# Three hand-written issue lists laid out anew, with the second layer's weights loaded at the head of the DMA queue

## The chip, the cores and the metric

The kernel runs on one core of a Trainium2 chip. A core has five engines with instruction queues of their own: TensorE (PE; its weight loads are shown as PEld), VectorE (DVE), ScalarE (ACT), GpSimd (POOL) and SyncE (SP, which here only issues DMAs). Each runs its instructions in the order in which the program hands them over, and semaphores between the queues hold an instruction back until what it reads is there and what it overwrites has been read. The metric is the device time of one execution in microseconds; lower is better. The time of a kernel is the median of its runs.

## The reference

`x` is 16 x 512 x 512 (16 batches, 512 tokens, width 512), in float32. For each token three tables are looked up by index, and three conditions per batch go through a small two-layer network. Cut to what is computed:

```
h = ln(x, pw_g[pathway], pw_b[pathway]);  h = ln(h, cp_g[comp], cp_b[comp])
t = ln(x, tm_g[time], tm_b[time]);        s = ln(x, ms_g[scale], ms_b[scale])
m, n, r = x + mlp_ln(memory), x + mlp_ln(noise), x + mlp_ln(resource)      # one row per batch
w = softmax(aw)
cat = concat([w0*h, w1*t, w2*m, w3*n, w4*r, w5*s])                         # 16 x 512 x 3072
out = x + ln(silu(cat @ int_W1 + int_b1) @ int_W2 + int_b2, int_g, int_be)
```

`ln` is a layer norm with mean and variance over the 512 columns.

## The kernel before

The 8192 tokens are sorted by the pair (compartment, scale) and cut into 16 tiles of 512 tokens (four rows of 128, counted 0 to 3). Because tokens of one row mostly share their pair, the time and scale norms are folded into one product: the first layer becomes a sum of three products per row instead of six. They read `catX` (x turned, block X), `catV` (the normalised x turned, block V, against weights `vs` built for the row's pair), and `catH` (the pathway and compartment part, block H). The products of X and H are done by a seven-product scheme on halves (names `m7.tile.pair.k`; sums in `token_sum`), except for tile 0, which multiplies plainly (`lX`, `lV`, `lH`). A row that holds a border between two pairs gets an extra product against the difference (names `ex` for the product, `ey`/`ez` for turning its rows, `ea`, `ee`, `eo` for gathering, adding and writing the result). The second layer uses the seven products `q7`. Results are gathered and scattered with indirect DMAs on POOL, since tokens are sorted.

The order of the work is written out by hand. `ctx.enter_context(tc.manual_schedule())` (L642) means that every engine's queue has its instructions in program order, and the program order is that of three lists of piece names: `ORDER` (L21 to L44, tile 0 and what is done once), `WINDOW` (L47 to L62, run for tiles 0 to 14, with `p`, `c`, `n`, `m` for the tile before, this one, the next and the one after) and `LAST` (L64 to L78). `run` (L1463) goes through a list and calls each piece once; a piece that `ORDER` has done already for tile 0 or 1 is skipped in `WINDOW`. The setup code ahead of `ORDER` (indices, one-hot products for the sort, loads) has an order of its own, which is not touched. Where a list puts a piece ahead of another changes the order only on the engines that both use.

Pieces that the change or the prediction names, with their engine:

- `lw` (SP, `load_w2`, L1403): loads `int_W2`, 1 MB, into the tile `w2`. The tile holds the condition networks' first weights until then; they are read by the setup's products of L844. `lt`, `lh`, `lo` (SP, L1098 to L1106): loads of three small tables, of the first layer's H block into `wh_` (1 MB; `wh_` holds a condition weight until `h2.2` has read it) and of three vectors to all partitions. `do`, `ro` (SP): write the difference rows and the bias rows to DRAM, where the gathers find them.
- `h2`, `he`, `eh` (PE, ACT, PE), `cs`, `cp`, `cn`, `ct`, `ca`, `cm`, `cr`, `rp`, `rc`, `ro`: the condition networks' second layer, its norm, and the bias rows made of it. `tb` (PE): products of the tables with the weights, `wh_` among them.
- `wm` and `wl` (ACT): means of the second layer's weights, and their subtraction. `wz`, `wq` (DVE): sums of half weights for the seven-product schemes. `wh` (ACT): scales `wh_`.
- `g4` and `g6` (POOL, L987, L1002), `g5` (PE and ACT, L997), `bx`/`by`, `kd`, `gt`, `tk`, `xa`: find the extra rows and their tokens.
- per row: `gx`, `gh`, `gc`, `gr`, `ga` (POOL, gathers of x, of `pw` rows, of `cp` rows, of difference rows and of bias rows), `xs` (sums of a row of x), `f1`, `fs`, `fv`, `fp`, `f2`, `fn` (DVE, ACT, DVE, POOL, DVE, ACT: the two norms of block H; `f2` reads the `cp` rows), `nv` (ACT, the normalised x), `mt` (DVE, times the difference row), `sp` and `bd` (ACT and DVE, build `vs` for a row), `tx`, `tv`, `th`, `tz` (DVE, transposes), `sX`, `sV`, `sH`, `sZ` (SP, four DMAs of 64 KB each that spread a transposed row over the partitions), `xt`, `vt`, `ht` (PE, the transposes of tile 0) with `xv`, `vv`, `hv` (copies out of PSUM).
- `ha`, `hs` (DVE, ACT: first layer's end), `zs` (POOL, sums for the second layer), `kb` (ACT, puts the bias into PSUM), `kf`, `ku` (ACT) and `sf`, `sl` (DVE) take the second layer's products out of PSUM, `lq`, `lv`, `lp`, `lb` the last norm, `po` (POOL) the output's scatter. `e1` (ACT, L590): a first square root, ahead of those of the last tile.

The two `cp`-tagged buffers of the pool `gp` go round over `gc` and `gr` in the order of the list, so a gather waits until the piece that read its buffer two places earlier is done (`gc.0.1` for `ey.1`, for example).

Of the kernel before, what the change touches and what calls it, by code (L numbers as in the profile page):

```python
# [1537 lines left out]
```

## Time and profile before

| | |
|---|---|
| runs of the kernel | 930.51, 933.6, 935.81 us; median 933.6 |
| the profiled execution | 930.14 us, of which the span is 928.4 us |
| busy time of the span | PE 892.2 us, DVE 735.6, POOL 651.7, ACT 521.2 |
| from HBM and back | 100.48 MB read, 19.97 MB written |

A row of a timeline gives the start (us from the span's start), the time it covers, engine, line, operation, destination <- sources, shape and, in brackets, how long the engine was idle before it and what ended that. `xN` counts records: a float32 matmul leaves two. A line of the waits gives the engine, the tile and line that waited, what it waited for, the sum in us, how often, and the longest. A row of the windows gives the stretch, its length, the busy time of PE, PEld, DVE, ACT and POOL with the number of records, the granted clock of PE, the share of the 16 DMA engines, and GB/s. Where a helper records every operation, the lines are the helper's.

### The profile page before, as it was taken

How to read it: one execution, taken by the hardware profiler on the slowest of the kernel's cores; microseconds unless marked ns; L12 is line 12 of the kernel's file. 1: busy time of each engine (PE TensorE's matmuls, PEld its weight loads, DVE VectorE, ACT ScalarE, POOL GpSimd, SP SyncE). 2: the span in 40 equal slices, each digit the busy share in tenths (PEclk: the TensorE clock that was granted, in tenths of full speed). 3: DMA queues.
4: the chain of work that ended last, by engine and by line, in shares of the span. 5: the costliest groups of instructions: out<-in, count | busy, mean ns of one | idle time of the engine just before them, and what ended most of it. 6: DMA issues, size and time to landing. Idle time of an engine off the chain costs nothing. (4 is left out here: it accounts for less than half of the span.)

```text
span 928.4 us, 13749 instructions
## 1 busy us (share of the span) xinstructions
PE 892.2 (96%) x3617; PEld 642.1 (69%) x3617; DVE 735.6 (79%) x1360; ACT 521.2 (56%) x1261; POOL 651.7 (70%) x730
## 2 busy tenths in 40 slices
...
GB/s 277 224 142 226 191 263 191 194 217 193 243 177 232 202 208 195 214 199 207 204 201 243 175 243 190 222 188 220 182 209 200 200 229 182 224 198 167 168 37 111
DMA packets 88557, 185.40 MB, mean 200 GB/s; under 512 B 24324, under 2 KB 24388, under 8 KB 88476
## 3 DMA queue, kind: packets, MB, share of 16 engines
...
q14 instruction: 51, 0.42, 0.2%
q10 hardware_dynamic: 704, 0.08, 0.1%
HBM read 100.48 MB, written 19.97 MB: 130 GB/s over the span
## 5 line engine op out<-in xcount | busy, mean ns | idle before, releaser
L404 PE MATMUL p<-vs,catV 128*128 128x512 f32 x512 | 228.0, 593 | 0.9 <-PEq L1363 0.6
L404 PEld LDWEIGHTS p<-vs,catV 128*128 128x128 f32 x512 | 96.7, 190 | 104.6 <-issue 101.9
L452 PE MATMUL p<-wh__81,catH 128*128 128x256 f32 x480 | 111.1, 379 | 0.0
L376 ACT ACTIVATE pw<-pw,rsh 128x512 f32<-128x512 f32 x64 | 45.7, 718 | 101.4 <-issue 45.1
L452 PEld LDWEIGHTS p<-wh__81,catH 128*128 128x128 f32 x480 | 91.2, 190 | 12.4
L475 ACT ACTIVATE add<-add 128x512 f32<-128x512 f32 x64 | 40.2, 631 | 97.6 <-DVE add L472 74.8
L171 POOL DMA_INDIRECT xbs<-in_x,tok x64 | 68.0, 1063 | 35.6 <-DVE yb L634 19.6
L638 POOL DMA_INDIRECT out<-yb,tok x64 | 66.5, 1039 | 31.6 <-issue 17.9
L391 POOL TENSOR_TENSOR xbs<-xbs,rows 128x512 f32<-128x512 f32 x64 | 82.1, 1285 | 1.3
L171 POOL DMA_INDIRECT pw<-in_pw,i_pw x64 | 64.2, 1003 | 26.0 <-DVE rH L197 12.8
L171 POOL DMA_INDIRECT add<-rows,i_add x64 | 69.2, 1082 | 15.6 <-issue 15.6
L171 POOL DMA_INDIRECT cp<-cp_rows,i_cp x64 | 67.5, 1054 | 17.7 <-issue 14.3
L383 DVE SCALAR_TENSOR_TENSOR pw<-pw,sumsh,cp 128x512 f32<-128x512 f32 x60 | 43.9, 753 | 43.8 <-DMA cp<-cp_rows,i_cp 43.6
L350 ACT ACTIVATE junk<-pw 128x512 bf16<-128x512 f32 x60 | 37.7, 628 | 71.3 <-DVE pw L347 30.2
L346 DVE SCALAR_TENSOR_TENSOR pw<-xbs,sums,pw 128x512 f32<-128x512 f32 x60 | 59.9, 998 | 13.7 <-DMA pw<-in_pw,i_pw 11.2
L625 POOL TENSOR_TENSOR rsy<-vey,mhalf 128x4 f32<-128x4 f32 (+1 forms) x16 | 21.6, 1348 | 64.4 <-DVE vey L620 64.4
L317 ACT ACTIVATE xm<-xbs,nmx,rsx 128x512 f32<-128x512 f32 x64 | 48.9, 808 | 26.6 <-issue 21.4
L612 ACT ACTIVATE junk<-yb 128x512 bf16<-128x512 f32 x64 | 40.2, 628 | 38.2 <-DVE yb L576 27.9
L452 PE MATMUL u<-wt,catX 128*128 128x256 f32 x240 | 56.6, 379 | 0.4 <-DVE add L463 0.4
L452 PE MATMUL u<-wx__80,ss 128*128 128x256 f32 x240 | 56.7, 379 | 0.0
L452 PE MATMUL p<-wt,catH 128*128 128x256 f32 x240 | 56.7, 379 | 0.0
L452 PE MATMUL u<-wt,ss 128*128 128x256 f32 x240 | 56.7, 379 | 0.0
...
## 6 DMA issues: line engine op xcount, KB each, us to landing
...
```

What stands on the lines that cost most here:

```text
L171: nc.gpsimd.indirect_dma_start(dst, None, table, bass.IndirectOffsetOnAxis(ap=idx, axis=0), **kw)
L317: nc.scalar.activation(t, st["xb"][:, j, :], AF.Identity, bias=st["nm"][:, j : j + 1], scale=st["rs"][:, j : j + 1])
L346: nc.vector.scalar_tensor_tensor(h, st["xb"][:, j, :], st["sums"][:, 1, j : j + 1], h, ALU.add, ALU.mult)
L350: nc.scalar.activation(junk, x, AF.Identity, accum_out=sums[:, 0, k : k + 1])
L376: nc.scalar.mul(pw[:, :D], pw[:, :D], st.pop(("rs", j)))
L383: nc.vector.scalar_tensor_tensor(pw[:, :D], pw[:, :D], st["sh", j][:, 1], cp, ALU.add, ALU.mult)
L391: nc.gpsimd.tensor_add(st["xb"][:, j, :], st["xb"][:, j, :], rows[:, 2, :])
L404: nc.tensor.matmul(st["p1", g], st["c" + blk][:, g, c, :], m[:, c, :], start=(blk == first and c == order[0]), stop=(blk == last and c == ...
L452: nc.tensor.matmul(dst, m[:, c], at_["half1"][k][:, c], start=(k == 1 and c == 0), stop=(c == NC - 1), skip_group_check=True)
L475: nc.scalar.activation(st["add", g], st["add", g], AF.Silu)
L612: nc.scalar.activation(junk, yb[:, j, :], AF.Square, accum_out=st["ssy"][:, j : j + 1])
L638: nc.gpsimd.indirect_dma_start(out_rows[j], bass.IndirectOffsetOnAxis(ap=tok[:, j, w : w + 1], axis=0), yb[:, j, :], None)
```

## The change

All three lists hold the same names as before (380, 197 and 189), each once; only their order is new. No function is changed.

On SP, `lw` is now the first piece of `ORDER`, ahead of `lt`, `lh`, `lo`, `do` and `ro`; before, it stood behind both `ro`. `lh` now stands ahead of `lo`. On PE the order of tile 0 is now

```
before: sz h2.2 ax h2.1 h2.0 g5 eh.2 xt.0.1 dp xt.0.0 bx eh.0 cv xt.0.3 xt.0.2 eh.1 tb lX.0.0 vt.0.2 vt.0.1 ct
        lX.0.1 vt.0.0 cm vt.0.3 ht.0.0 rp.1 rp.0 ey.0 lV.0.1 ey.1 ht.0.2 ex.0 ey.2 lX.0.2 ex.2 ht.0.1 ey.3 ex.1 ...
after:  h2.0 h2.1 h2.2 ax sz xt.0.1 eh.2 eh.0 dp g5 xt.0.2 bx eh.1 xt.0.0 cv tb xt.0.3 vt.0.1 ct vt.0.2 vt.0.0
        cm ht.0.0 lX.0.0 rp.0 rp.1 vt.0.3 lX.0.1 ht.0.2 ey.0 lX.0.2 ey.1 ex.0 ey.2 lV.0.1 ex.1 ht.0.1 ey.3 ex.2 ...
```

On POOL, `g6` now stands ahead of `g4`, and the gathers `ea.1`, `ea.2` of the extras come earlier among the others. In `WINDOW`, on ACT `kf.p.1` stands ahead of `ku.p.0`, on DVE `sf.p.1` ahead of `sf.p.0`; on POOL `zs.p.0` stands behind `ga.c.2` and `fp.c.3`; on SP the rows of the next tile go `sV.n.3 sV.n.0 sV.n.2 sX.n.2 sX.n.0 sV.n.1 sX.n.1 sX.n.3`, where it was `sV.n.1 sV.n.0 sV.n.3 sV.n.2 sX.n.2 sX.n.0 sX.n.1 sX.n.3`. In `LAST`, the second layer's last products go 5, 7, 1, 6, 4, 2, 3 where it was 1, 7, 2, 5, 3, 6, 4, and `e1` stands behind the third root of the last tile. The diff, cut:

```diff
 ORDER = """
-    wk.1.3 se g4 fg wk.1.0 sz h2.2 ax wk.2.3 wk.1.1 pwi lt h2.1 h2.0 he.2 tt scl lo lh wk.2.1 pk xs.0.1 dk xs.0.3
-    wk.1.2 he.0 g5 eh.2 xt.0.1 dp g6 fl.3 he.1 dc xt.0.0 bx eh.0 cv xt.0.3 xt.0.2 eh.1 by xv.0.1 sp.0.1 xv.0.3
-    xv.0.2 ac xv.0.0 kd xs.0.0 xs.0.2 wk.2.2 cg wk.2.0 xe.0 cs gh.0.0 gt.0.3 gt.0.1 gt.0.2 gt.0.0 gh.0.2 xp.0
-    gc.0.0 cp f1.0.0 xm.0 tk.0 nv.0.2 fl.2 wm.4 nv.0.1 tb lX.0.0 vt.0.2 fl.0 vt.0.1 nv.0.0 nv.0.3 vv.0.1 vv.0.2
-    gx.e0.0 gt.1.3 gx.e0.1 gt.1.1 fs.0.0 cn f1.0.2 gt.1.0 gx.e0.2 ct fs.0.2 do xs.e0.0 gt.1.2 gx.e0.3 lX.0.1
-    vt.0.0 fl.1 ca fv.0.2 fv.0.0 cw tk.1 f2.0.0 vd.1 bd.0.1 gx.e1.2 gx.e1.3 gc.0.2 gr.e0.0 fp.0.2 gx.e1.1 fp.0.0
-    xs.e0.1 cm vt.0.3 xs.e0.2 xs.e0.3 fn.0.0 f2.0.2 xa.1 xe.e0 gr.e0.1 xp.e0 xm.e0 cr ht.0.0 rp.1 nv.e0.0 vv.0.3
-    vv.0.0 rc.1 ro.1 xa.0 xs.e1.1 va.0 mt.e0.0 hv.0.0 gh.0.1 gx.e1.0 rp.0 gx.1.0 ey.0 lV.0.1 nv.e0.1 rc.0 ar
-    mt.e0.1 xs.e1.0 fn.0.2 xs.e1.2 ez.0 nv.e0.2 nv.e0.3 xs.e1.3 ey.1 ht.0.2 gr.e0.2 f1.0.1 tx.1.0 xe.e1 mt.e0.2
-    fs.0.1 wl.4 sp.0.3 ex.0 ey.2 wb ro.0 lw sp.0.0 fv.0.1 gx.1.1 hv.0.2 ez.2 lX.0.2 ex.2 gc.0.1 ea.0 gx.1.2 gx.1.3
-    fp.0.1 gr.e0.3 gh.0.3 f2.0.1 ee.0 tx.1.1 bd.0.0 vd.0 mt.e0.3 eo.0 gc.0.3 xp.e1 va.1 fn.0.1 ez.1 xs.1.2 ht.0.1
-    ey.3 f1.0.3 fs.0.3 f2.0.3 xm.e1 fv.0.3 ea.2 gr.e1.0 ea.3 gr.e1.2 ea.1 gh.1.3 fp.0.3 ea.5 xs.1.3 ez.3 xs.1.0
-    xs.1.1 nv.e1.2 nv.e1.0 xe.1 ee.2 bd.0.3 mt.e1.0 mt.e1.2 ex.1 ey.6 ex.3 ey.4 ez.6 nv.e1.3 wm.0 nv.e1.1 ez.4
...
+    g6 fg wk.1.3 wk.1.0 g4 h2.0 h2.1 wk.1.1 dk lw h2.2 fl.1 xs.0.0 ax sz se wk.2.1 xs.0.2 wk.1.2 pwi he.1 he.0
+    he.2 xt.0.1 lt xs.0.1 wk.2.3 scl eh.2 eh.0 dp xs.0.3 lh gh.0.0 tt fl.2 xe.0 g5 lo xt.0.2 fl.3 gh.0.2 xp.0 bx
+    eh.1 xt.0.0 cv by xv.0.2 dc kd xm.0 wk.2.2 cs gt.0.0 gt.0.1 gt.0.3 gt.0.2 cp f1.0.0 fs.0.0 fv.0.0 cn cg nv.0.1
+    wm.4 nv.0.2 xv.0.0 sp.0.1 tb xt.0.3 vt.0.1 fl.0 ct vt.0.2 ca gt.1.3 gc.0.0 fp.0.0 tk.0 cw wk.2.0 f1.0.2 f2.0.0
+    nv.0.0 xv.0.3 ac vv.0.2 nv.0.3 xv.0.1 wl.4 fn.0.0 va.1 gx.e0.0 gx.e0.1 xa.0 xs.e0.0 pk vt.0.0 gt.1.2 gt.1.0
+    gx.e0.2 gx.e0.3 do gc.0.2 cm cr xs.e0.1 ht.0.0 lX.0.0 rp.0 rp.1 vt.0.3 xs.e0.2 xs.e0.3 hv.0.0 bd.0.1 fs.0.2
+    fv.0.2 f2.0.2 xe.e0 gt.1.1 gr.e0.0 gh.0.1 fp.0.2 gr.e0.1 xp.e0 tk.1 xm.e0 rc.0 fn.0.2 rc.1 nv.e0.0 nv.e0.1
+    mt.e0.0 f1.0.1 mt.e0.1 lX.0.1 ht.0.2 nv.e0.2 wh nv.e0.3 ey.0 ez.0 vv.0.0 gx.e1.3 gx.e1.1 ro.0 wb vv.0.1 ar
+    fs.0.1 gx.1.0 gr.e0.2 gx.1.2 gx.e1.0 xa.1 vd.0 lX.0.2 xs.e1.1 ey.1 mt.e0.2 vv.0.3 ro.1 xs.e1.0 ex.0 ea.0
+    gc.0.1 gx.e1.2 xs.e1.2 sp.0.0 xs.e1.3 ez.1 gx.1.3 xe.e1 fv.0.1 ee.0 gh.0.3 ey.2 fp.0.1 gr.e0.3 gx.1.1 xp.e1
+    bd.0.0 f2.0.1 tx.1.0 f1.0.3 mt.e0.3 tx.1.3 fs.0.3 tx.1.2 xs.1.2 xs.1.3 va.0 ez.2 fn.0.1 gc.0.3 eo.0 lV.0.1
+    ex.1 ht.0.1 ey.3 xm.e1 hv.0.2 fv.0.3 f2.0.3 gr.e1.0 ea.1 ea.2 gh.1.3 gr.e1.2 fp.0.3 nv.e1.0 xs.1.0 ez.3 xs.1.1
+    wm.0 fn.0.3 nv.e1.2 vd.1 ee.1 mt.e1.0 xe.1 mt.e1.2 hv.0.1 ex.2 ey.6 ex.3 ey.4 ez.6 nv.e1.1 nv.e1.3 wm.1
...
 WINDOW = """
-    kz.p.2 kz.p.1 ha.p.2 f1.c.2 kb.p.2 kz.p.0 ga.c.2 tz.p.3 lV.c.1 lV.c.0 m7.c.1.1 m7.c.0.1 kb.p.1 sh.c.1 kb.p.0
-    gc.c.2 gc.c.3 sp.c.3 hs.p.2 tz.p.2 bd.c.3 f1.c.3 fs.c.2 sp.c.2 xs.n.0 fs.c.3 fv.c.2 bd.c.2 f2.c.2 fv.c.3
-    f2.c.3 sZ.p.0 sZ.p.1 sZ.p.2 fp.c.2 ga.c.0 zs.p.0 fp.c.3 lV.c.3 q7.p.0.1 q7.p.0.2 q7.p.0.7 xs.n.1 fn.c.2 fn.c.3
-    kf.p.0 xs.n.2 zs.p.1 zs.p.2 q7.p.0.5 q7.p.0.6 ku.p.0 kf.p.1 tx.n.1 th.c.2 th.c.3 tx.n.3 r1.c.0 sZ.p.3 gh.n.0
-    zs.p.3 zs.p.4 sf.p.0 tx.n.2 sf.p.1 zs.p.5 xs.n.3 zs.p.6 q7.p.1.2 vd.n tx.n.0 r1.c.1 xe.n xp.n ga.c.1 ga.c.3
-    sH.c.3 sh.c.2 zs.p.7 sH.c.2 kz.p.3 q7.p.1.1 sl.p.0 sH.c.0 sH.c.1 q7.p.0.3 q7.p.0.4 kb.p.3 kf.p.2 va.n sf.p.2
-    sl.p.1 xm.n q7.p.1.5 q7.p.1.7 nv.n.1 nv.n.3 lq.p.0 kf.p.3 f1.n.0 tv.n.3 tv.n.1 sf.p.3 q7.p.1.6 lV.c.2 q7.p.1.4
...
-    m7.c.0.4 m7.c.0.3 fs.n.1 sp.n.0 fn.n.0 f2.n.1 r5.c.1 fv.n.1 r3.c.0 th.n.0 r2.c.1 ha.c.1 lb.p.3 ha.c.0 m7.c.1.7
-    m7.c.1.4 gx.m.2 gx.m.0 po.p.0 gx.m.1 sh.c.0 fp.n.1 po.p.1 gh.n.2 sh.c.3 po.p.2 hs.c.1 hs.c.0 fn.n.1 tz.c.1
-    r3.c.1 tz.c.0 th.n.1 ha.c.3 sV.n.1 sV.n.0 sV.n.3 sV.n.2 sX.n.2 sX.n.0 sX.n.1 gh.n.3 gx.m.3 sX.n.3 hs.c.3
-    po.p.3 bd.n.0
+    kz.p.1 lV.c.1 lV.c.0 kz.p.0 kz.p.2 ha.p.2 gc.c.2 f1.c.2 tz.p.3 kb.p.0 kb.p.1 kb.p.2 sh.c.1 gc.c.3 ga.c.0
+    m7.c.0.1 m7.c.1.1 sp.c.3 hs.p.2 tz.p.2 bd.c.3 f1.c.3 fs.c.2 xs.n.0 sp.c.2 fs.c.3 fv.c.2 f2.c.2 bd.c.2 fv.c.3
+    f2.c.3 sZ.p.0 sZ.p.1 sZ.p.2 fp.c.2 ga.c.2 fp.c.3 zs.p.0 lV.c.3 q7.p.0.2 q7.p.0.1 q7.p.0.7 fn.c.2 xs.n.1 fn.c.3
+    kf.p.0 zs.p.1 zs.p.2 q7.p.0.5 q7.p.0.6 q7.p.1.2 q7.p.1.1 xs.n.2 kf.p.1 r1.c.0 tx.n.1 th.c.2 th.c.3 tx.n.3
+    tx.n.0 ku.p.0 sf.p.1 sf.p.0 gh.n.0 zs.p.3 sZ.p.3 zs.p.4 zs.p.5 tx.n.2 vd.n r1.c.1 xs.n.3 sH.c.1 zs.p.6 kz.p.3
+    sH.c.2 sH.c.0 xe.n sl.p.0 xp.n ga.c.3 ga.c.1 sh.c.2 zs.p.7 sH.c.3 q7.p.0.4 q7.p.0.3 kb.p.3 va.n kf.p.2 sf.p.2
+    sl.p.1 xm.n f1.n.0 q7.p.1.5 q7.p.1.7 q7.p.1.6 lV.c.2 nv.n.1 nv.n.3 kf.p.3 tv.n.1 tv.n.3 sf.p.3 q7.p.1.4
...
+    m7.c.1.5 m7.c.0.5 m7.c.0.6 m7.c.1.6 m7.c.0.4 m7.c.0.3 f1.n.1 lb.p.0 lb.p.2 lb.p.1 r5.c.0 r2.c.0 r5.c.1 u4.c.1
+    f2.n.0 m7.c.0.7 fs.n.1 fn.n.0 ha.c.0 r2.c.1 th.n.0 r3.c.0 f2.n.1 fv.n.1 ha.c.1 lb.p.3 m7.c.1.3 m7.c.1.7
+    m7.c.1.4 po.p.0 gx.m.2 sh.c.0 po.p.1 gx.m.0 gh.n.2 fp.n.1 po.p.2 sh.c.3 hs.c.0 hs.c.1 fn.n.1 sp.n.0 tz.c.1
+    th.n.1 r3.c.1 gh.n.3 sV.n.3 sV.n.0 sV.n.2 sX.n.2 sX.n.0 sV.n.1 tz.c.0 ha.c.3 sX.n.1 gx.m.3 gx.m.1 sX.n.3
+    hs.c.3 bd.n.0 po.p.3
 LAST = """
...
-    m7.c.0.4 m7.c.0.3 q7.p.1.1 q7.p.1.7 q7.p.1.2 q7.p.1.5 r3.c.1 ha.c.2 r3.c.0 ft.p.1 ha.c.1 ha.c.3 ha.c.0 hs.c.2
-    hs.c.3 hs.c.1 hs.c.0 kf.p.2 kf.p.3 tz.c.3 tz.c.1 e0 tz.c.2 tz.c.0 sf.p.3 sf.p.2 ft.p.0 po.p.1 zs.p.6 zs.p.7 w2
-    po.p.0 sZ.c.0 q7.p.1.3 q7.p.1.6 q7.p.1.4 l2.c.0 e1 ku.p.1 sl.p.2 sl.p.3 yg.p.2 yg.p.3 la.c.0 lq.p.3 lq.p.2
-    sd.p.3 sd.p.2 lq.c.0 sd.c.0 sZ.c.1 sZ.c.3 sZ.c.2 rv.p.2 ft.p.2 rv.p.3 yg.c.0 rv.c.0 ft.p.3 ft.c.0 l2.c.1
-    l2.c.3 l2.c.2 po.p.2 po.p.3 sh.c.2 po.c.0 la.c.1 lq.c.1 sd.c.1 yg.c.1 rv.c.1 ft.c.1 la.c.3 la.c.2 lq.c.2
-    sd.c.2 lq.c.3 sd.c.3 po.c.1 yg.c.2 rv.c.2 ft.c.2 rv.c.3 yg.c.3 ft.c.3 po.c.2 po.c.3
...
+    m7.c.0.4 m7.c.0.3 q7.p.1.5 q7.p.1.7 q7.p.1.1 r3.c.1 ha.c.2 ft.p.0 r3.c.0 ft.p.1 ha.c.3 ha.c.1 ha.c.0 hs.c.3
+    hs.c.2 hs.c.1 hs.c.0 kf.p.2 kf.p.3 tz.c.3 tz.c.1 e0 tz.c.0 tz.c.2 sf.p.3 w2 po.p.1 sh.c.3 zs.p.7 po.p.0 sZ.c.0
+    q7.p.1.6 q7.p.1.4 q7.p.1.2 q7.p.1.3 l2.c.0 ku.p.1 sl.p.2 sl.p.3 sf.p.2 yg.p.3 yg.p.2 la.c.0 lq.p.3 lq.p.2
+    sd.p.3 sd.p.2 lq.c.0 sd.c.0 sZ.c.2 sZ.c.1 sZ.c.3 rv.p.2 rv.p.3 ft.p.2 rv.c.0 ft.p.3 yg.c.0 ft.c.0 l2.c.2
+    l2.c.1 l2.c.3 po.p.2 po.p.3 po.c.0 la.c.2 la.c.1 lq.c.1 sd.c.1 lq.c.2 sd.c.2 rv.c.1 yg.c.1 ft.c.1 la.c.3
+    yg.c.2 yg.c.3 rv.c.2 ft.c.2 e1 lq.c.3 sd.c.3 po.c.1 rv.c.3 ft.c.3 po.c.2 po.c.3
...
```

37 lines of the change are left out of this document (18 added, 19 removed).

## The prediction

> **What bounds the kernel now.** I read the page first, for the span, and then the busy time of the engines in three stretches: the rest of the start behind the setup code (38 to 78 and 78 to 120 us, where the list ORDER runs) and the long stretch in which the windows run. Columns: PE, PEld, DVE, ACT and POOL busy, granted clock, DMA share, GB/s.
>
> ```profile
> span 928.4 us, 13749 instructions
> ```
>
> ```profile
> 38.00:78.00 40.00, 35.86 (x228) 18.04 (x227) 30.69 (x99) 25.81 (x70) 29.28 (x34) 0.91 0.50 155
> 78.00:120.00 42.00, 35.49 (x95) 16.01 (x95) 28.13 (x53) 29.84 (x66) 25.97 (x27) 0.92 0.74 233
> 120.00:905.00 785.00, 777.65 (x3051) 575.85 (x3049) 634.04 (x1129) 439.43 (x1057) 555.75 (x569) 1.00 0.72 200
> ```
>
> From 120 us on PE is idle for 7.35 of 785 us at the full clock: nothing that only changes an order can win more than that there, and since no operation goes, PE's work stays. The start is different: PE is idle 4.1 us in the first of its stretches and 6.5 us in the second, at clocks of 0.91 and 0.92. Next, whom PE waited for over the whole run, and PE's timeline where the long waits lie.
>
> ```profile
> PE px L1350 <- DVE pre L1343: 3.4, 1, 3.4
> PE ptH L1201 <- ACT pw L376: 3.1, 2, 2.2
> PE pq_0b L546 <- DVE yb L565: 2.5, 12, 0.2
> PE pq_0b L546 <- POOL yb L532: 2.1, 4, 0.8
> PE px L1350 <- issue: 1.4, 1, 1.4
> ...
> PE pq_1b L546 <- DVE yb L565: 1.1, 1, 1.1
> PE ptH L1201 <- DMA adde<-rows,i_x: 0.9, 1, 0.9
> ```
>
> ```profile
> 94.58 0.66 PE L1201 MATMUL ptH<-ident,pw 128*128 128x128 f32 x4 [0.84 <-ACT pw L376]
> 98.59 1.11 PE L1350 MATMUL px<-ident,pre 128*128 128x128 f32 x4 [3.36 <-DVE pre L1343]
> 99.50 5.55 PE L1365 MATMUL pe<-wt,catZ 128*128 128x512 f32 x8
> 105.48 3.67 PE L1365 MATMUL pe<-wt,catZ 128*128 128x512 f32 x8 [0.42 <-PEq L1348]
> ...
> 125.94 14.28 PE L404 MATMUL p<-wh__81,catH 128*128 128x512 f32 x32
> ```
>
> The pair 0.84 and 3.36 us is one event, and its cause is read from the queues: SP's timeline, POOL's, and DVE's.
>
> ```profile
> 35.37 0.51 SPq L1053 DMA_DIRECT2D in_order<-catZ  x1
> ...
> 41.78 0.37 SPq L1103 DMA_DIRECT2D wh__81<-in_int_W  x1
> ...
> 81.58 0.40 SPq L1404 DMA_DIRECT2D w<-in_int_W  x1
> ```
>
> ```profile
> 82.63 0.95 POOL L171 DMA_INDIRECT cp<-cp_rows,i_cp  x1 [0.83 <-PE ptH L1201]
> ```
>
> ```profile
> 92.88 0.75 DVE L381 SCALAR_TENSOR_TENSOR pw<-pw,sumsh,cp 128x512 f32<-128x512 f32 x1 [4.93 <-DMA cp<-cp_rows,i_cp]
> ...
> 95.24 2.70 DVE L265 SCALAR_TENSOR_TENSOR vs<-wt,sct,vs 128x512 f32<-128x512 f32 x4
> 97.85 0.69 DVE L1343 TENSOR_TENSOR pre<-xme,pre 128x512 f32<-128x512 f32 x1
> ```
>
> The second layer's weights (lw, 1 MB) go out at 81.58 us. The gather of the `cp` rows (gc.0.1) is issued at 82.63 and its first reader (f2.0.1) starts at 92.88, after 4.93 us in which DVE did nothing. Behind it in DVE's order stand a weight build (bd.0.0, 2.70 us) and the product that ey.3 transposes (97.85 us), so PE loses 0.84 us at ht.0.1 and 3.36 us at ey.3. The DMA share and the clock (last three columns) in slices of 2 us:
>
> ```profile
> 36.00:38.00 2.00, 2.00 (x38) 1.10 (x35) 0.55 (x4) 1.98 (x4) 0.44 (x3) 1.00 0.31 24
> ...
> 52.00:54.00 2.00, 2.00 (x8) 0.80 (x7) 1.64 (x11) 2.00 (x5) 0.97 (x1) 0.56 0.69 252
> ...
> 90.00:92.00 2.00, 2.00 (x6) 0.91 (x5) 0.00 (x0) 0.00 (x0) 1.56 (x2) 1.00 0.91 348
> ...
> 98.00:100.00 2.00, 1.41 (x5) 1.25 (x6) 1.95 (x3) 0.79 (x3) 0.10 (x1) 0.50 0.10 39
> ```
>
> While the gather is late the DMA engines are full (348 GB/s); at 36 to 38 us they move 24 GB/s. Behind the idle 3.36 us the clock is 0.50.
>
> **The change part by part.** *lw moves* from behind the bias rows (ro) to the head of SP's list. It needs only that the first condition products (L844) have read the same buffer, long past, so it goes out behind the L1053 issue, at about 36 us. It is one issue (0.40 us on SP) and 1 MB: 3.0 us at the 348 GB/s of the full row, so landed near 40 us. It passes lt, lo, lh, do and both ro on SP's queue. The three lt loads are short and wait 0.40 us more. The gathers of the first tile's x are issued from 38 us on, so at most 2 us of the transfer meet them; I take nothing, and 2 us as the upper end. lh still waits for h2.2 and now stands ahead of lo; its tile is read here:
>
> ```profile
> 57.35 0.63 PE L1264 MATMUL pb<-wh__81,room 128*32 128x512 f32 x3
> ```
>
> That is 15.6 us behind the 41.78 of the issue; two products ahead of h2.2 and the third megabyte take a third of it. Cover gone, each microsecond would be one of PE.
>
> [...]
>
> *What the move frees.* Without the megabyte beside it, and with the bias rows (ro) earlier too, gc.0.1 should land well inside its old 9.3 us (82.63 + 0.95 to 92.88). In the new list, from the end of ey.1 (which frees its buffer) PE has ex.0, lV.0.1 and ex.1 to do before ht.0.1, by the 14.28 us for four such blocks some 10.7 us. Against it stands the longer of two ways: the gather's issue and landing, or, on ACT and DVE, some copies, sp.0.0 (about as long as bd.0.0), bd.0.0 itself (2.70 us); then f2.0.1 (0.75 us) and one row operation of ACT. I put that at 8.5 us, an estimate, so slack of 2 us. ey.3 has under 1 us by the same count. I take both stalls as gone: 0.84 + 3.36 us. Then PE has no gap ahead of ex.1, which ran 5.55 us against the 3.67 us of its like: 1.9 us, and 0.45 us on ey.3's own transposes (1.11 against 0.66). The 0.9 us at ht.0.3 is late extra rows; the gathers ea.1 and ea.2 go earlier in the new list; I take 0.7 of it. The half microseconds that PE's sequencer spends on skipped blocks stay. Sum for 78 to 120 us: −(0.84 + 3.36 + 1.9 + 0.45 + 0.7) = −7.3 us; bounds −9 (all of the idle time and the clock's loss) and +1.
>
> [...]
>
> *The rest of ORDER, to 78 us.* One move speaks against the change: g6 now stands ahead of g4 on POOL.
>
> ```profile
> 46.91 2.54 POOL L1003 TENSOR_SCALAR room<-room,off 14x896 f32<-14x896 f32 x1
> ```
>
> So the segment rows come 2.54 us later, and PE's g5, with everything PE has behind it (bx, eh.1, xt.0.0, the table products), waits up to that long. For it: fn.0.0 goes ahead of the extras' sums on ACT, where ht.0.0 waited 2.2 us; the extra products' chain (cm, cr, rp) starts before lX.0.0 and lX.0.1 instead of behind; ht.0.2 goes ahead of ey.0, where PE stood 1.4 us. But ht.0.0 now stands ahead of both lX, with less of PE's work to hide f2.0.0. I take 0, with −3 (the 2.2 and part of the 1.4) and +3 (the 2.54 and a little) as ends.
>
> *WINDOW*, 14 full times. kf.p.1 and sf.p.1 go ahead of ku.p.0 and sf.p.0, so the half that PE overwrites next is read one ACT copy and one DVE sum sooner: the 12 waits on L565 go, −2.5 us. zs.p.0 now stands behind ga.2 and fp.3 on POOL; it waits for the spread of Z anyway, which hides both; cover gone, the 2.1 us on L532 grow. Bounds −4.5 and +3.
>
> In SP's list V's row 1, which PE reads first in the next window, becomes the sixth of eight rows instead of the first:
>
> ```profile
> 523.04 10.02 SPq L205 DMA_DIRECT2D catV<-rV  x16
> 533.16 14.03 SPq L205 DMA_DIRECT2D catX<-rX  x16
> ```
>
> ```profile
> 545.76 2.74 PE L404 MATMUL p<-vs,catV 128*128 128x512 f32 x6
> ```
>
> At 10.02/16 = 0.63 us each the 24th transfer is issued 15 us behind 523.04, at 538 us; PE reads row 1 at 545.76. Some 5 us of slack are left after the landing: no cost.
>
> *LAST.* The end's 1.1 us on L565 halves, since products 1, 6 and 4 now stand between 5 and 3, but 6 then waits for ACT's copy: −0.5 us. The root's table load (e1) leaves its idle place:
>
> ```profile
> 901.90 1.28 ACT L592 ACT_TABLE_LOAD   x1
> ```
>
> It now falls on the roots of tile rows 2 and 3 of the tile before, whose outputs are not the last; hidden, 1.28 us if not. −0.5 us in all, bounds −1.5 and +1.3.
>
> **Sum:** −7.3 + 0 − 2.5 − 0.5 = −10.3 us on the profiled execution, which took 930.14 us (span 928.4 and 1.7 us around it): 919.8. The runs shown go from 930.51 to 935.81 with the median 933.6, so that execution is 3.5 us under the median; a median of new runs should stand above 919.8 by some of this. I take about a third, 921 us.
>
> **The rivals.**
>
> *The head is won and partly given back* where the next waits lie: tile 1's rows X and V stand in SP's list behind the extras' last rows (eo.4 to eo.7), and those behind POOL's gathers ea. If POOL, whose gathers cost about a microsecond each, comes no earlier than before, the 28 transfers behind eo (28 × 0.63 = 17.6 us) reach PE several microseconds late, and 3 to 6 us of the 10.3 return: 925. For it: POOL is busy 25.97 of 42 us without its gaps. Against: its waits there were for the same late gathers.
>
> *Nothing measurable:* the stalls at 94 to 99 us only move, because ey.3 has under 1 us of slack, or the 2.54 us of g6 reach ht.0.0 whole. Then 2.5 + 0.5 us are left, or less: 930 to 933, I say 931.
>
> *Slower:* V's row 1, now sixth. Its 5 us of slack hang on X's rows 2 and 0 being issued at once; if their wait for the token sums' readers holds the queue, each further microsecond is paid 14 times. Up to 5 us it costs nothing; with the start's gain spent, a delay of 6.5 us gives +21 − 10 = +11 us, 945. Against it: the 14.03 us for X's 16 rows hold 4 us of waiting in all, and these belong to the two rows that the last half products still read.
>
> **How the numbers follow.** Forecast 0.62, given back 0.18, nothing 0.12, slower 0.08. About 0.5% (4.7 us) is what a measurement of this kernel can tell from no change. The forecast is faster whole; of "given back" I count four fifths faster; of "nothing" all as same: faster 0.76, same 0.16, slower 0.08. The forecast's own range, with the bounds of its terms taken together, is 914 to 928; with the next two cases 913 to 932.
>
> **What would show it.** Right: no wait over 1 us at ey.3 (L1350) and none of DVE on `cp` near 80 to 95 us; the L404 block of 32 records on `wh` starting 6 to 11 us earlier than 125.94; no row of L546 waiting 12 times for L565; the clock 1.00 where it was 0.50. Wrong: PE waits for the gathers of x (L171) before 50 us; a wait of L404 on `catV` in every window; the block on `wh` where it was, or the gap between it and the first half products grown.

## The result, and the profile after

The changed kernel takes 921.85 us (median of four runs from 921.23 to 922.6); the kernel before, beside it, 932.06 (928.84 to 935.81). The ratio is 0.989, with a 95% interval from 0.985 to 0.993: 10 us less, the predicted time within 1 us. The profiled execution took 922.05 us. The sum came out; two of its terms were mis-sized and a third was missing, so part of the nearness is luck. The windows of the changed kernel, with the columns of the prediction:

```profile
span 920.3 us, 13553 instructions
```

```profile
38.00:78.00 40.00, 36.81 (x235) 17.56 (x234) 30.13 (x93) 27.46 (x72) 30.65 (x35) 0.87 0.63 201
78.00:120.00 42.00, 39.44 (x107) 17.86 (x108) 32.92 (x69) 33.64 (x71) 32.16 (x32) 1.00 0.74 220
```

From 78 to 120 us PE is busy 39.44 us instead of 35.49, at the full clock instead of 0.92. The waits of PE over the whole run:

```profile
PE pq_0b L546 <- POOL yb L532: 4.3, 5, 1.6
PE pt L1295 <- issue: 2.0, 1, 2.0
PE p L404 <- DVE vs L265: 1.7, 1, 1.7
PE pq_0a L546 <- ACT yb L556: 1.2, 1, 1.2
...
PE ptH L1201 <- DVE pw L346: 0.8, 1, 0.8
...
PE px L1350 <- issue: 0.5, 1, 0.5
```

The 3.4 us at L1350 (ey.3), the 3.1 us of L1201 on ACT's `pw` and the 12 waits on L565 are gone, as forecast. Not in the sum: L532 grew from 2.1 to 4.3 us, and 2.0, 1.7 and 1.2 us are new.

To see where the time went, every trace is cut into four stretches by five points: the issue of L1053 on SP (the last of the setup, at 34.90 to 35.96 us in the 14 traces), the start of the block on `wh` (L404), the start of the second window's first block on `vs`, the start of the last block (L487), and the end. Before, from SP's and PE's timelines (the other two points of before stand in the prediction):

```profile
191.15 7.03 PE L404 MATMUL p<-vs,catV 128*128 128x512 f32 x16
241.59 7.03 PE L404 MATMUL p<-vs,catV 128*128 128x512 f32 x16
...
905.22 13.97 PE L487 MATMUL p<-w,catV 128*128 128x512 f32 x32
```

After:

```profile
35.87 0.51 SPq L1053 DMA_DIRECT2D in_order<-catZ  x1
```

```profile
118.84 14.28 PE L404 MATMUL p<-wh__81,catH 128*128 128x512 f32 x32
...
144.46 3.67 PE L404 MATMUL p<-vs,catV 128*128 128x512 f32 x8 [0.37 <-issue]
...
152.80 1.10 PE L546 MATMUL pq_0a<-w2t,yb 128*128 128x256 f32 x4 [1.22 <-ACT yb L556]
...
185.88 7.03 PE L404 MATMUL p<-vs,catV 128*128 128x512 f32 x16
235.87 7.03 PE L404 MATMUL p<-vs,catV 128*128 128x512 f32 x16
...
896.96 13.97 PE L487 MATMUL p<-w,catV 128*128 128x512 f32 x32
```

| stretch, us | before | after | difference |
|---|---|---|---|
| start: L1053 to the block on `wh` | 90.57 | 82.97 | −7.60 |
| first window, from there | 65.21 | 67.04 | +1.83 |
| the windows behind it, to L487 | 714.07 | 711.08 | −2.99 |
| the end | 23.18 | 23.34 | +0.16 |

These sum to −8.6; the setup ended 0.5 us later in this execution (35.87 against 35.37), and the spans differ by 8.1. The medians differ by 10.2.

### The profile page after: what moved, and what is told of

Read it like the earlier page. It is cut to its first block, busy times and chain, and to the rows that moved or that the text cites. A ratio compares the mean times of both kernels' runs of the same rounds, so it can differ in the third digit from the quotient of the medians.

```text
span 920.3 us, 13553 instructions
## 1 busy us (share of the span) xinstructions
PE 887.0 (96%) x3617; PEld 642.2 (70%) x3617; DVE 726.6 (79%) x1360; ACT 520.4 (57%) x1261; POOL 669.5 (73%) x730
## 5 line engine op out<-in xcount | busy, mean ns | idle before, releaser
L404 PE MATMUL p<-vs,catV 128*128 128x512 f32 x512 | 228.1, 593 | 4.0 <-DVE vs L265 1.7
L404 PEld LDWEIGHTS p<-vs,catV 128*128 128x128 f32 x512 | 96.6, 190 | 108.4 <-issue 100.8
L638 POOL DMA_INDIRECT out<-yb,tok x64 | 76.9, 1201 | 31.3 <-issue 15.1
L376 ACT ACTIVATE pw<-pw,rsh 128x512 f32<-128x512 f32 x64 | 45.6, 714 | 92.9 <-DVE pw L383 53.7
L171 POOL DMA_INDIRECT cp<-cp_rows,i_cp x64 | 74.4, 1162 | 14.5 <-issue 12.8
L625 POOL TENSOR_TENSOR rsy<-vey,mhalf 128x4 f32<-128x4 f32 (+1 forms) x16 | 23.6, 1474 | 83.1 <-DVE veh L368 70.1
L171 POOL DMA_INDIRECT xbs<-in_x,tok x64 | 66.0, 1031 | 22.0 <-issue 18.2
L171 POOL DMA_INDIRECT pw<-in_pw,i_pw x64 | 63.0, 984 | 25.1 <-issue 12.2
L171 POOL DMA_INDIRECT add<-rows,i_add x64 | 66.9, 1045 | 19.3 <-issue 19.3
L383 DVE SCALAR_TENSOR_TENSOR pw<-pw,sumsh,cp 128x512 f32<-128x512 f32 x60 | 45.6, 761 | 39.7 <-DMA cp<-cp_rows,i_cp 31.2
L372 POOL TENSOR_TENSOR rsh<-veh,mhalf 128x1 f32<-128x1 f32 x64 | 48.5, 758 | 14.9 <-DVE veh L368 11.6
L346 DVE SCALAR_TENSOR_TENSOR pw<-xbs,sums,pw 128x512 f32<-128x512 f32 x60 | 46.0, 767 | 12.5 <-DMA pw<-in_pw,i_pw 6.8
L452 PE MATMUL u<-wx__80,ss 128*128 128x256 f32 x240 | 54.5, 379 | 0.0
L452 PEld LDWEIGHTS u<-wx__80,catX 128*128 128x128 f32 x240 | 45.6, 190 | 12.7 <-issue 6.9
```

The costliest lines, as they stand in the source:

```text
L171: nc.gpsimd.indirect_dma_start(dst, None, table, bass.IndirectOffsetOnAxis(ap=idx, axis=0), **kw)
L346: nc.vector.scalar_tensor_tensor(h, st["xb"][:, j, :], st["sums"][:, 1, j : j + 1], h, ALU.add, ALU.mult)
L372: nc.gpsimd.tensor_tensor(rs, st.pop(("ve", j)), mhalf[:, :1], ALU.pow)
L376: nc.scalar.mul(pw[:, :D], pw[:, :D], st.pop(("rs", j)))
L383: nc.vector.scalar_tensor_tensor(pw[:, :D], pw[:, :D], st["sh", j][:, 1], cp, ALU.add, ALU.mult)
L404: nc.tensor.matmul(st["p1", g], st["c" + blk][:, g, c, :], m[:, c, :], start=(blk == first and c == order[0]), stop=(blk == last and c == ...
```

## The experiments

Each kernel has the same pieces in another order; all compute the whole result. The same four stretches, from one trace each, with the medians and ratios to the kernel before (95% interval). Times of before in these comparisons: 931.0 to 932.0. A trace is of a single execution; three of them lie 4 us or more from their medians: 940.52 us ("two swaps"), 935.47 ("zs.p.0 ahead") and 925.0 ("changed, again").

| kernel | median | ratio | start | first window | windows | end |
|---|---|---|---|---|---|---|
| before, `lw` first | 928.96 | 0.997 (0.995 to 0.999) | 84.8 | 65.2 | 718.7 | 23.1 |
| before, new ORDER | 930.24 | 0.998 (0.996 to 1.001) | 85.5 | 67.5 | 715.5 | 23.1 |
| before, new WINDOW and LAST | 925.64 | 0.992 (0.989 to 0.995) | 90.4 | 65.0 | 710.2 | 23.3 |
| before, two swaps | 932.17 | 1.002 (0.999 to 1.005) | 91.6 | 65.2 | 722.9 | 23.1 |
| before, POOL new | 949.7 | 1.020 (1.017 to 1.023) | 88.0 | 65.2 | 734.8 | 23.1 |
| changed, again | 920.62 | 0.988 (0.984 to 0.993) | 85.7 | 66.8 | 711.9 | 23.3 |
| changed, `lw` back | 925.69 | 0.991 (0.988 to 0.994) | 86.7 | 66.9 | 711.8 | 23.3 |
| changed, swaps undone | 920.51 | 0.986 (0.982 to 0.990) | 85.4 | 67.8 | 707.5 | 23.3 |
| changed, zs.p.0 ahead | 943.77 | 1.014 (1.009 to 1.018) | 82.0 | 66.4 | 726.1 | 23.3 |
| changed, POOL old | 959.21 | 1.030 (1.026 to 1.034) | 81.9 | 67.7 | 748.2 | 23.4 |
| changed, gx in order | 919.65 | 0.988 (0.984 to 0.993) | 82.0 | 66.5 | 710.1 | 23.4 |
| changed, gx, wl, wq early | 919.62 | 0.987 (0.983 to 0.990) | 85.6 | 66.4 | 706.9 | 23.3 |

### The weights' load alone

```diff
 ORDER = """
-    wk.1.3 se g4 fg wk.1.0 ...
+    lw wk.1.3 se g4 fg wk.1.0 ...
...
-    ... ey.2 wb ro.0 lw sp.0.0 ...
+    ... ey.2 wb ro.0 sp.0.0 ...
```

> The kernel before, with one item moved: lw stands first in ORDER. The prediction's theory (the second layer's megabyte held up the gather gc.0.1): DVE's wait for cp ahead of f2.0.1 shrinks from 4.93 us to under 1, the waits of 0.84 and 3.36 us at ht.0.1 and ey.3 go, the clock behind them stays at 1.00, and the first window's block on wh starts 4 to 6 us earlier than 125.94; time 4 to 6 us under the kernel before. Rival (the order of the lists did it, the megabyte's place is nothing): the 4.93 us stays above 3, the block stays within 1 us, time the same.

DVE's row of f2.0.1 and PE's of ey.3 in this trace:

```profile
87.99 0.81 DVE L381 SCALAR_TENSOR_TENSOR pw<-pw,sumsh,cp 128x512 f32<-128x512 f32 x1 [1.16 <-DMA cp<-cp_rows,i_cp]
```

```profile
94.67 0.66 PE L1350 MATMUL px<-ident,pre 128*128 128x128 f32 x4 [1.18 <-DVE pre L1343]
```

The reader is to see the 4.93 us of DVE shrink to 1.16 (a little over the microsecond expected) and the 3.36 of PE to 1.18 with nothing else changed; the start is 5.8 us shorter. Three more traces below have the old ORDER with the load in its old place: DVE's wait is 4.21 us in the one with the new WINDOW and LAST, and PE's at ey.3 is 2.4 to 2.9 us in all three. So the load did hold up the gather. The whole kernel wins only 3 us in the median, where 4 to 6 were expected: in the trace, the old windows took 4.6 us more than in the trace of before.

### The load back in its old place

```diff
-    g6 fg wk.1.3 wk.1.0 g4 h2.0 h2.1 wk.1.1 dk lw h2.2 ...
+    g6 fg wk.1.3 wk.1.0 g4 h2.0 h2.1 wk.1.1 dk h2.2 ...
...
-    ... ey.1 mt.e0.2 vv.0.3 ro.1 xs.e1.0 ...
+    ... ey.1 mt.e0.2 vv.0.3 ro.1 lw xs.e1.0 ...
```

> The changed kernel with one item moved back: lw behind ro.1, as before. The prediction's theory: the megabyte is issued near 81 us again and lies beside the gather gc.0.1; DVE waits for cp, PE waits at ht.0.1 or ey.3 for 2 to 5 us and the clock falls behind it; time 4 to 7 us above the changed kernel. Rival (the new order of the other items keeps the stall away by itself): no such wait, block on wh within 1 us of 118.84, same time.

3.8 us above the changed kernel's first median, 5.1 above its second: at the lower edge of the prediction's theory. From the first product of ey.0 to the block on `wh` this trace has 43.2 us, where all eight traces with the new ORDER and `lw` first have 40.7 to 41.0, so the rival (the order of the rest keeps the stall away) falls. The start of the block, 121.72 us, doesn't tell: a second trace of the changed kernel has it at 121.28. But the place is another, and PE does not wait at ht.0.1 or ey.3. The megabyte, issued at 77.89 us, now meets a gather of difference rows:

```profile
88.24 0.69 DVE L1343 TENSOR_TENSOR pre<-xme,pre 128x512 f32<-128x512 f32 x1 [3.33 <-DMA pre<-diff_rows,i_x]
```

The two runs together: of the start's gain either part alone takes more than half (−5.8 the load, −3.9 the rest without it, against the trace of before; −5.3 and −3.4 of −6.2 against the mean of four traces with the old ORDER, below). They overlap, since both shorten DVE's wait for the same gather, gc.0.1: 1.16 us are left with the load alone, none with the rest alone.

### The new ORDER alone, the new WINDOW and LAST alone

The kernel before with the whole new ORDER:

```diff
 ORDER = """
-    wk.1.3 se g4 fg wk.1.0 sz h2.2 ax wk.2.3 ...
...
+    g6 fg wk.1.3 wk.1.0 g4 h2.0 h2.1 wk.1.1 dk lw ...
...
```

> The kernel before with the new ORDER, lw's move in it, and the old WINDOW and LAST. The theory that follows from the trace of after (start worth 7.6 us, first window gives 1.8 back, the other windows win 3.0): if the 1.8 us belong to the start, the block on wh starts near 118.8 and the time is 5 to 6 us under before; if they belong to the new WINDOW, the time is 7 to 8 us under before. The waits of 0.21 us on L565 are there again, the waits on L532 return to some 2 us in all.

The kernel before with the whole new WINDOW and LAST:

```diff
 WINDOW = """
-    kz.p.2 kz.p.1 ha.p.2 f1.c.2 kb.p.2 kz.p.0 ga.c.2 ...
...
+    kz.p.1 lV.c.1 lV.c.0 kz.p.0 kz.p.2 ha.p.2 gc.c.2 ...
...
 LAST = """
-    kb.p.0 gc.c.2 lV.c.1 ga.c.2 gc.c.3 ...
...
+    ha.p.2 gc.c.2 kb.p.1 kb.p.0 ga.c.0 ...
...
```

> The kernel before with the new WINDOW and LAST and the old ORDER. By the prediction: 3.0 us less than before, all from the 12 waits on L565 and half of the 1.05 us at the end. By the trace of after: some 1 us less, as PE's waits for POOL on L532 grow from 2.1 to 4.3 us; if the first window's loss of 1.8 us hangs on the new start, up to 3 us less. The start up to 125.94 us stays as it was.

This turned the shares round. ORDER alone is worth 1.8 us in the median, with an interval that reaches zero; neither of the two forecasts made for it (5 to 6, 7 to 8 us) held. The two other lists alone are worth 6.4 us, twice the forecast. The traces give the new ORDER more than its median does (−6.2 us at the start and +1.8 in the first window, by the means below); the difference stays open. The first window's +1.8 belongs to the new ORDER: every trace with it has 66.4 to 67.8 us there, every trace without it 65.0 to 65.2.

Why the windows are worth more than the sum of their shown waits is read in PE's timeline of before, around one of the 12 waits:

```profile
209.22 1.89 PE L546 MATMUL pq_1a<-w,catZ 128*128 128x256 f32 x8
211.32 1.10 PE L546 MATMUL pq_0b<-w,yb 128*128 128x256 f32 x4 [0.21 <-DVE yb L565]
212.26 1.03 PE L546 MATMUL pq_0b<-w2t,catZ 128*128 128x256 f32 x4
213.12 1.03 PE L546 MATMUL pq_1b<-w,catZ 128*128 128x256 f32 x4
```

Undisturbed, four records take 0.86 us from start to start (212.26 to 213.12), so eight take 1.73. Here the eight take 2.10 (209.22 to 211.32): 0.37 us lost, where the bracket says 0.21, because the bracket counts from the shown end of the last matmul (209.22 + 1.89 = 211.11), and a shown end overlaps its successor when nothing stalls (212.26 + 1.03 = 213.29, where the next starts at 213.12). The four behind the wait take 0.94 instead of 0.86. One wait costs 0.45 us. The starts of whole windows say the same: 241.59 − 191.15 = 50.44 before, 235.87 − 185.88 = 49.99 after. Twelve such waits are 5.4 us, not 2.5; this is an estimate from one wait and one pair of windows.

### What removes the waits on L565: the two swaps

In the kernel before:

```diff
 WINDOW = """
-    ... q7.p.0.6 ku.p.0 kf.p.1 tx.n.1 ... sf.p.0 tx.n.2 sf.p.1 ...
+    ... q7.p.0.6 kf.p.1 ku.p.0 tx.n.1 ... sf.p.1 sf.p.0 tx.n.2 ...
```

> The kernel before with two swaps in WINDOW and nothing else: kf.p.1 ahead of ku.p.0 (ACT), sf.p.1 ahead of sf.p.0 (DVE). By the prediction's count (0.21 us per wait on L565, 12 times) the time falls by 2.5 us and the time from one window's first block to the next goes from 50.44 to 50.23. By the starts of the matmuls around the wait (0.37 us between two where 0.22 is the step, and a slower group behind it) each wait costs 0.45: 50.44 becomes 50.00 and the eight undisturbed windows together are 3.6 us shorter. Both: no wait on L565 is left.

The opposite, in the changed kernel:

```diff
 WINDOW = """
-    ... kf.p.1 ... tx.n.0 ku.p.0 sf.p.1 sf.p.0 gh.n.0 ...
+    ... tx.n.0 ku.p.0 kf.p.1 sf.p.0 sf.p.1 gh.n.0 ...
```

> The changed kernel with the two swaps in WINDOW undone: ku.p.0 ahead of kf.p.1 on ACT, sf.p.0 ahead of sf.p.1 on DVE. If the swaps are needed for the gain: some 12 waits of 0.2 us on L565 are back, the quiet step from window to window is 50.4 instead of 50.0 and the time 3 to 6 us above the changed kernel (0.45 us for each wait). Rival (the gain comes from the other moves in WINDOW alone, as the kernel before with only the swaps did not become faster): quiet step 50.0 to 50.1, time within 2 us of the changed kernel.

Neither run bears out that the swaps are what pays. With the swaps in the kernel before, the 12 waits on L565 go, and the kernel is no faster (1.002). In its trace, which is of one of its slowest executions (940.52 us of 929.0 to 941.07), PE waits in the next places instead, two of them here.

```profile
226.20 1.99 PE L452 MATMUL u<-wx__80,ss 128*128 128x256 f32 x8 [0.60 <-DVE ss L433]
260.76 1.13 PE L546 MATMUL pq_0b<-w2t,yb 128*128 128x256 f32 x4 [1.17 <-POOL yb L532]
```

With the swaps undone in the changed kernel the waits stay away, and it is as fast as with them. DVE's timeline shows what differs, first before:

```profile
209.83 0.42 DVE L563 TENSOR_TENSOR yb<-yb,pq_0a 128x256 f32<-128x256 f32 x1 [1.80 <-ACT yb L569]
210.16 0.70 DVE L197 STREAM_TRANSPOSE rX<-xbs 128x512 f32<-128x512 f32 x1
210.79 0.38 DVE L565 TENSOR_TENSOR yb<-yb,pq_0b 128x256 f32<-128x256 f32 x1
```

Then in the changed kernel with the swaps undone:

```profile
206.84 0.38 DVE L563 TENSOR_TENSOR yb<-yb,pq_0a 128x256 f32<-128x256 f32 x1
207.15 0.41 DVE L565 TENSOR_TENSOR yb<-yb,pq_0b 128x256 f32<-128x256 f32 x1
```

Between sf.p.0 (L563) and sf.p.1 (L565) stood a transpose, tx.n.2; it puts L565 0.63 us later (210.16 to 210.79), more than the loss of 0.45. In both of these kernels it stands behind the pair, and in neither does L565 hold PE up in this place: above, L565 ends at 207.56, and PE overwrites the half at 207.91 without a wait. So with the transpose out of the way the swaps aren't needed. Whether the swaps would do with the transpose left between the sums is not shown, since the kernel with the two swaps moves sf.p.1 past it too. The quiet windows of the kernel with the swaps undone take 50.0 to 50.3 us.

### POOL's order: one piece, all of it, and its counterpart

One piece of the changed kernel's WINDOW moved back:

```diff
 WINDOW = """
-    ... fp.c.2 ga.c.2 fp.c.3 zs.p.0 lV.c.3 ...
+    ... fp.c.2 zs.p.0 ga.c.2 fp.c.3 lV.c.3 ...
```

> The changed kernel with zs.p.0 back ahead of the gather ga.c.2 and fp.c.3 in WINDOW. Rival to the prediction's working: its place behind the two is why PE's waits on L532 grew, so they fall from 4.3 to some 2 us in all and the time by 2 us. The prediction's own cover (POOL waits there for the spread of Z anyway): L532 stays at 3 to 5 us in all, in the last five windows alone, and the time does not fall; ga.c.2, now behind a wait, may come late and cost up to 1 us per window.

All of POOL's pieces of WINDOW put in the old order, in the changed kernel (the others stay; POOL's alone are shown):

```diff
 WINDOW = """
-    gc.c.2 sh.c.1 gc.c.3 ga.c.0 fp.c.2 ga.c.2 fp.c.3 zs.p.0 ... po.p.0 gx.m.2 sh.c.0 po.p.1 gx.m.0 ...
+    ga.c.2 sh.c.1 gc.c.2 gc.c.3 fp.c.2 ga.c.0 zs.p.0 fp.c.3 ... gx.m.2 gx.m.0 po.p.0 gx.m.1 sh.c.0 ...
```

> The changed kernel with POOL's items of WINDOW in the order of before (ga.c.2 first, zs.p.0 ahead of fp.c.3, and so on), every other engine as in the changed kernel. If the new order of POOL is needed: PE waits for L532 or L534 in most windows and the time is 3 us or more above the changed kernel. Rival (it doesn't matter which of the two orders POOL has as long as ga.c.2 stands ahead of zs.p.0): quiet step 50.0 to 50.1, time within 2 us of the changed kernel.

And all of them put in the new order, in the kernel before:

```diff
 WINDOW = """
-    ga.c.2 sh.c.1 gc.c.2 gc.c.3 fp.c.2 ga.c.0 zs.p.0 fp.c.3 ... gx.m.2 gx.m.0 po.p.0 gx.m.1 sh.c.0 ...
+    gc.c.2 sh.c.1 gc.c.3 ga.c.0 fp.c.2 ga.c.2 fp.c.3 zs.p.0 ... po.p.0 gx.m.2 sh.c.0 po.p.1 gx.m.0 ...
```

> The kernel before with POOL's items of WINDOW in the new order and nothing else changed (the counterpart of the run with POOL's old order in the changed kernel). If POOL's order by itself carries the gain (the puts stand ahead of the gathers of x that wait for DVE, so POOL runs ahead and the Z rows come earlier): POOL's wait for DVE's yb (12.3 us between 190 and 590 us) is under 4, SP's wait for rZ falls from 29.1 to under 20, the 12 waits on L565 stay and the quiet step stays 50.44, and the time is 2 to 4 us under the kernel before. If the orders only work together: PE waits for POOL on L532 or L534 in half of the windows or more, and the time is 3 us or more above it.

These are the largest effects of all: 22 to 23 us slower for one piece moved over two (943.77), 37 to 39 for POOL's old order in the changed kernel (959.21), 19 for the new one in the kernel before (949.7). For the one piece neither expectation held: the time rose by more than 1 us per window, and PE's waits on L532 fell from 4.3 to 1.2 us, while new ones came on L534. POOL's rows in the first of the three, in one window:

```profile
248.75 0.72 POOL L532 TENSOR_TENSOR yb<-catZ 128x256 f32<-128x256 f32 x1 [3.04 <-DMA catZ<-rZ]
249.63 1.01 POOL L171 DMA_INDIRECT add<-rows,i_add  x1 [0.17 <-issue]
250.68 0.58 POOL L372 TENSOR_TENSOR rsh<-veh,mhalf 128x1 f32<-128x1 f32 x1
251.22 0.72 POOL L534 TENSOR_TENSOR catZ<-catZ 128x256 f32<-128x256 f32 x1
```

POOL waits 3.04 us for the spread of Z, and only then does ga.c.2 (L171) and fp.c.3 (L372), which would have fitted into the wait; the second sum (L534) comes 1.7 us late, and PE waits for it:

```profile
PE pq_0b L546 <- POOL catZ L534: 13.6, 12, 3.7
```

So the cover that the prediction named is there, and it is worth a great deal: work ahead of zs.p.0 is free here, work between the sums is not. The trace is of the fastest of this kernel's five executions, 935.47 us where the other four have 941.9 to 945.46; its windows are 15.0 us longer than those of the changed kernel's first trace. By an estimate, 13.6 us of waits at 0.24 more each (0.45 for a shown 0.21, above) are 16.5, less the 3.1 gone from L532: some 13, most of what this execution lost. What the slower four lost beyond it no trace shows.

In the two crossed kernels each engine waits for the other's old place. POOL's and SP's waits between 190 and 590 us, before:

```profile
SPq L205 <- DVE rZ L197: 29.1, 8, 4.3
```

after:

```profile
SPq L205 <- DVE rZ L197: 15.7, 5, 4.4
```

changed, POOL old:

```profile
SPq L205 <- DVE rZ L197: 51.2, 8, 7.1
```

before, POOL new:

```profile
POOL out L638 <- DVE yb L634: 27.0, 7, 4.7
```

In the last, the scatter po.p.0 stands first among the tile's ends, as the new order of DVE has it, but the old order of DVE gets to its row (lb.p.0) late; POOL stands up to 4.7 us with the x gathers behind it, and 27.0 us in all, where the changed kernel has 3.2 (3 times). In the kernel with POOL's old order the `pw` rows come late for DVE (L346 waits 19.7 us for them; 2.0 in the changed kernel), so, as I read these sums, the Z rows come late for SP, then for POOL, then for PE: L532 10 times, 9.8 us in all. Half the new order is worse than none of it. My expectation of 2 to 4 us from POOL's order alone fell; its rival, that the orders only work together, held in the time. SP's wait for rZ, which I expected under 20 us there, is 33.8. PE does wait for POOL on L532 in 8 windows, but these waits come to 3.3 us; in this kernel PE waits longer for DVE:

```profile
PE p L404 <- DVE vs L265: 4.5, 3, 1.6
PE u L452 <- DVE add L463: 4.0, 5, 0.9
PE pq_0b L546 <- POOL yb L532: 3.3, 8, 0.7
```

### A second trace, and the loss in the first window

The changed kernel was timed and traced once more:

> The changed kernel once more, for a second trace of it. Every theory: 920 to 924 us. What it tells apart: if the start up to the block on wh is again 82.5 to 83.5 us long behind the issue of L1053, that is the new ORDER's; if it is 85 or more as with the old WINDOW behind it, single executions differ by 2 us there and one trace cannot fix the start's share.

The time is the same (920.62); the start is 85.7 us and the block on `wh` begins 4.7 us earlier than before, not 7.1, so one trace does not fix the start's share. Over all eight traces with the new ORDER and `lw` first it is 81.9 to 83.0 (four) or 85.4 to 85.7 (four), with mean 83.9; over four with the old ORDER 88.0 to 91.6, mean 90.1. What the two groups go with stands in the last section.

The next two ask where the first window's 1.8 us went. First, POOL's gathers of the third tile's x, in the changed kernel:

```diff
 ORDER = """
-    gx.2.1 ... gx.2.2 ... gx.2.3 gx.2.0
+    gx.2.0 ... gx.2.1 ... gx.2.2 gx.2.3
```

> The changed kernel with the gathers of the third tile's x, in ORDER, in the order 0 1 2 3 instead of 1 2 3 0; nothing else moves. Theory: the 1.8 us that the first window lost come from gx.2.0, issued last, on whose rows ACT waits (xs.n.0) ahead of the copy of the first half products (kf.p.0); with it first, ACT's wait of 6.53 us shrinks, the waits near 152 us go, and the stretch from the block on wh to the second window's first block falls from 67.04 us to 65.0 to 65.6; time 1 to 2 us under the changed kernel. Rival (the Z rows or the DMA load at that time are late): the stretch stays at 66.5 to 67.5.

Then the same, and beside it wl.1 (ACT) and wq (DVE) earlier:

```diff
 ORDER = """
-    ... wl.3 wl.2 nv.1.3 ... wz f1.1.0 ... wl.1 ... th.1.1 th.1.0 ... wq
+    ... wl.3 wl.2 wl.1 nv.1.3 ... wz wq f1.1.0 ... th.1.1 th.1.0 ...
```

> The changed kernel with three moves at the end of ORDER: gx.2.0 first as before, wl.1 directly behind wl.2 on ACT and wq directly behind wz on DVE. Theory for what is left of the first window's loss (DVE works off wq, 3.5 us, ahead of the branch that lets PE start lV.c.3): wq fills the 3.1 us in which DVE waits for the pw rows, so DVE reaches the branch some 3 us earlier, the wait of 1.27 us at 144.5 goes and the stretch from the block on wh to the second window's first block is 65.0 to 65.6 us instead of 66.5; time 1 us under the kernel with gx alone. Rival (the rows of V and X come late there): the wait stays, now for a DMA.

In the changed kernel gx.2.0 is the last of the four gathers, and its sums (xs.n.0) stand first on ACT, ahead of the copy kf.p.0. ACT's row there, after:

```profile
148.62 0.63 ACT L350 ACTIVATE junk<-xbs 128x512 bf16<-128x512 f32 x1 [6.53 <-DMA xbs<-in_x,tok]
```

With the gathers in order that row starts at 141.86, and PE's wait at 152.80 is gone; but the stretch shrinks only by 0.55 us, because the wait at 144.46 grows:

```profile
144.53 3.67 PE L404 MATMUL p<-vs,catV 128*128 128x512 f32 x8 [1.27 <-ACTq L248]
```

DVE ended wq at 144.37, just before, and its branch for this block stands behind it; with wq moved into an idle stretch of DVE that wait is gone too. Then the next one shows:

```profile
152.45 1.13 PE L546 MATMUL pq_0b<-w2t,yb 128*128 128x256 f32 x4 [1.18 <-POOL yb L532]
```

Each cause was real and each was covered by the next: in both the stretch is 66.4 to 66.5 us, not the 65.0 to 65.6 of both theories; the second trace of the changed kernel has 66.8 with no move at all. What is left, the Z rows' arrival, was not taken away. The two kernels' medians, 919.65 and 919.62, are 1 to 2 us under the changed kernel's, which these runs can't tell from no difference.

## Why the prediction was right, point by point

*78 to 120 us, −7.3.* Right against the execution it was made for: from the first product of ey.0 to the block on `wh` that trace has 48.1 us (77.86 to 125.94), and all eight traces of the new ORDER with `lw` first have 40.7 to 41.0, so −7.2. Of the old ORDER's typical start it was too much: three more traces of it have 45.2 to 46.1 us there, so the mean is 46.2 and the gain 5.4. The profiled execution was the worst of the four in this stretch, and one trace doesn't tell that: its wait at ey.3 is 3.36 us where the others have 2.4 to 2.9, and the clock is 0.50 for 6.8 us beside it (96.6 to 103.4); the block behind it takes 5.55 us, 5.16 to 5.35 in the others. No wait of DVE on `cp` is left near 80 to 95 us; the slack claimed for ht.0.1 and ey.3 held in both traces of the changed kernel.

*lw at no cost.* Held: PE's wait for the x gathers is nothing in the first trace of the changed kernel and 0.45 us in the second, inside the 2 us named as the upper end.

*ORDER to 78 us, 0 (−3 to +3).* Held. g6 ahead of g4 did move g5 back (13.1 us behind L1053 instead of 11.0), but ey.0 came 42.1 us behind it instead of 42.5. Over all traces it comes at 41.0 to 44.8 with the new ORDER and at 42.4 to 45.5 with the old, means 43.0 and 43.9.

*WINDOW, −2.5.* The sign and the 12 waits were right; the term was mis-sized. Each wait was worth 0.45 us and not 0.21, by the estimate above. And three traces with the old list have 714.1, 718.7 and 715.5 us in this stretch, six with the new (the three kernels with single moves that change it left out) 706.9 to 711.9: means 716.1 and 710.3, so 5.8 us. The step "the half that PE overwrites is read one copy and one sum sooner" left out a move: the transpose between the two sums goes too, and with it gone the swaps aren't needed. "Hidden by the spread of Z" was right for zs.p.0's new place. L532 did grow, to 4.3 us; why is not shown. Its five waits (352, 656, 709, 760 and 811 us) come 5 to 16 us behind the starts of five rebuilds of `vs` on DVE (347.5, 639.9, 698.9, 751.1, 801.8), though three more rebuilds behind 340 us (364.3, 668.9, 853.3) have no such wait of their own; one pair, after:

```profile
698.88 2.88 DVE L265 SCALAR_TENSOR_TENSOR vs<-wt,sct,vs 128x512 f32<-128x512 f32 x4
```

```profile
708.91 1.13 PE L546 MATMUL pq_0b<-w2t,yb 128*128 128x256 f32 x4 [1.61 <-POOL yb L532]
```

My reading is that in these windows PE, now earlier, runs into Z rows that DVE has held up; it was not tried.

*LAST, −0.5.* The 1.05 us at the last half products became 0.60 in every kernel with the new list. This wait lies ahead of L487, so its gain is part of the 5.8 us; the stretch behind L487 grew by 0.16 us. The root's table load (1.28 us) cost nothing at the end.

*What the sum left out* is the first window: +1.8 us (65.2 to 67.0). PE reaches it 7 us earlier, DVE reaches the end of ORDER 6.0 us earlier (wq at 140.77 instead of 146.77), and ACT, POOL and the Z rows behind them are late by the difference. With `lw` alone PE comes 6.2 us earlier (119.70), its first half products too (148.22 instead of 154.46) with no wait ahead of them, and the stretch stays at 65.2 us. One of the prediction's own signs of being wrong did appear here: the gap from the block on `wh` to the first half products grew, from 28.5 to 29.1 us. The rival "head won, partly given back" saw such a loss, but placed it in the queue behind eo. Together, by means: −6.2 + 1.8 − 5.8 + 0.2 = −10.0, where the forecast was −7.3 + 0 − 2.5 − 0.5 = −10.3. The head fell short by as much as the windows were better: that the errors cancel is luck. The windows' means rest on three and six traces that spread by 4.6 and 5.0 us.

*The rivals.* V's row 1 as the sixth costs nothing: no wait of L404 on `catV` is in the list of after. "Nothing measurable" needed ey.3 to stall again; it did so only without the other moves (1.18 us with `lw` alone).
